# A two-layer graph network on one core: last keys on both array halves, moments from every other row tile, score rows by transfers

## The chip, the cores and the metric

The kernel runs on one core of a Trainium2 chip. The metric is device time of one execution in microseconds, the median of several runs. The engines are named as in the profile: PE is the matrix engine (PEld its weight loads, which can lie beside matmuls), DVE the vector engine, ACT the scalar engine, POOL the general engine, SP the engine whose queue issues most transfers. Each engine works through its own queue in order.

## The reference, cut to what matters

There are N = 3327 nodes with 256 features. The adjacency is dense in memory and mostly zeros.

```python
# layer 0: h = relu(layernorm(x)), then
R = adj + eye; R = R / R.sum(-1)
for n in range(2):
    logits = (Xa @ W1.T @ W2.T) @ (Xa @ W3.T).T          # queries and keys have 64 features
    probs  = softmax(logits)
    A  = probs kept from the largest down while the sum of those before is < 0.9, renormalized
    Xf = R @ Xf
    Xa = A @ Xa
    Z += Xf @ U1[n].T + Xa @ U2[n].T
x = x + layernorm(h + Z)
# layer 1: h = relu(layernorm(x)), hp = h @ W as 4 heads of 64
e    = leaky_relu(s[:, None] + d[None, :], 0.2)          # s, d: one score per node and head
attn = softmax(where(adj > 0, e, -inf))
x = x + elu(attn @ hp)
```

## The kernel before

Rows are cut into NT = 26 tiles of 128 (the last has 127 real rows, NP = 3328 with padding). Everything is float32; a float32 matmul shows as two records in the trace, a transpose as one. No order is written by hand: `Plan` (line 470) holds every piece of work with its engine, an assumed length, a rank (due time), what it needs, and which buffers it takes and gives. `Plan.order` (line 497) plays this through once: a free engine takes the ready piece of the lowest rank whose buffers are free. The pieces are then issued in the order found, each on its engine's queue. So any changed piece or length gives a new order everywhere.

The stages are these.

Preparation (`prepare`, line 1094): each row tile is loaded, normalized, transposed and projected into keys and queries (`wqk`). Keys lie in `kt`, transposed, 64 features on one half of the partitions; `half_of` (line 620) puts four tiles on the one half, the next four on the other, and so on. A row's queries lie in `qq` on both halves. So two logits matmuls of 64 partitions each can work on both halves of the array at once. Tiles 24 and 25, the last, are both on half 0. `project_u` (line 1149) multiplies by U1 ahead of the sums.

`moments` and `keys_summed` (lines 725, 1087): the sum and second moment of the keys, from which a row's mean and variance of logits follow. For each of 26 key tiles: a transpose (L733), an ACT copy (L737), a matmul of 65 columns (L742), two DVE additions into `gk` (L754). `scaled` divides by N, `stats` (line 758) takes each row's mean and variance.

Steps n = 0 and 1, ranks 0 and 30: per row tile, `search` (line 1350) with class `Row` (line 816) computes logits in two pieces (columns 0 to 2047, and 2048 to 3326 as a pair of 512 and one matmul of 255 on half 0, L845), exponentials on ACT (L856) into a buffer `e` of the pool of four, a first threshold from the moments, and two (step 0) or three (step 1) counts over the row (L893) that move the threshold. The number of counts is fixed. Then come a window, a sort and the choice on DVE. `attention` (line 1402) transposes `e` and multiplies (L1016, L1028). Column 3327 of `e`, the padding, is set to zero by POOL (L833) when the buffer is opened. `full` (line 1417) multiplies the row tile of R (loads of four adjacency tiles into one of four buffers `at`, L1049; matmuls L1060 from `main` or `c`); it is the filler of PE's queue. `finish1` (line 1162) makes the next step's keys, `finish2` (line 1251) the second layer's features and scores: `main[:, t]`, `sd`, `qd`, `low`. `failures` (line 1331) marks rows whose choice can't be trusted; one such row makes the whole program run again on the slow path `general`.

Neighbour stage (`attend_neighbours`, line 1440, ranks 60 to 99): four blocks b of W = 832 destination nodes. For each of the 26 source tiles j: the adjacency is loaded (L1513), turned into a bf16 mask in an `et` buffer (L1523, L1524), DVE multiplies the larger of two exponentials by the mask for each of four heads (L1535) into one of six buffers (four `e`, two in the memory of `rhs`), and PE multiplies (products L1551, denominators L1565, three tiles at a time). The scores of the destination nodes are broadcast to all partitions (`broadcast`, L1473 and L1477): for each tile and head a transpose of the score column seen as 128 equal columns, then an exponential into `both`, which lies in the memory of `c` and so needs all full sums of step 1 done (`opened`). Each block ends in `leave` (L1605, L1608), transposes (L1626), division, elu and the store.

## Time and profile before

| | us |
|---|---|
| median of 3 runs | 2272.42 (2270.28 to 2273.19) |
| profiled execution | 2271.77 |
| its span | 2269.9 |
| PE busy | 2207.6 |
| DVE busy | 1618.2 |
| ACT busy | 1480.0 |
| POOL busy | 915.3 |

A line of the profile's groups names the line of the kernel, the engine, the operation, what is written and read, how often, and then busy time, the mean of one in ns, and the idle time just before it with what ended that. Matmuls overlap, so the mean of one is longer than the distance from one to the next; the latter is what a queue can gain. Seen over the span, the preparation takes the first 60 us, step 0 lies up to some 940, step 1 up to some 1757, then the neighbour stage until 2247.6 and the output's end.

### The profile page before, as it was taken

The page shows a single profiled execution, that of the slowest core. Times are in us where ns is not written, and L with a number is a line of the kernel's source. Part 1 is how long each engine was busy: PE and PEld are TensorE (multiplying, and loading weights), DVE is VectorE, ACT ScalarE, POOL GpSimd, SP SyncE. Part 2 cuts the span into 40 slices and gives each one's busy share as a digit, 9 for nine tenths or more (in the row PEclk, how much of TensorE's full clock was granted, in tenths as well). Part 3 has the DMA queues.
Part 4 walks back from the last instruction along what each step waited for, and adds up shares of the span by engine and source line. Part 5 has one row for each costly group of instructions (what it writes and reads, how often), then busy time and mean ns, then how long its engine had stood idle before and what let it go on. Part 6 is the DMA issues. An engine that isn't in the chain of part 4 may idle for free. (4 is left out here: it accounts for less than half of the span.)

```text
span 2269.9 us, 36125 instructions
## 1 busy us (share of the span) xinstructions
PE 2207.6 (97%) x11956; PEld 1547.5 (68%) x11956; DVE 1618.2 (71%) x4273; ACT 1480.0 (65%) x2849; POOL 915.3 (40%) x2263
## 2 busy tenths in 40 slices
PE   7999999999999999999999999999999999999997
PEld 5477778777877778877878777878788433343332
DVE  5576656557565562277878898678776898989895
ACT  5766686677666851478887877777872646565553
POOL 6455555546533540256646656665561000000000
PEclk9999999999999999999999999999999999999998
DMA  3011221212212222531222122222222443434341
GB/s 98 20 37 53 83 69 53 64 51 61 74 48 74 69 82 76 183 86 54 65 57 73 56 61 70 70 75 75 67 74 78 119 118 107 120 106 120 102 126 42
DMA packets 189653, 176.96 MB, mean 78 GB/s; under 512 B 14866, under 2 KB 145808, under 8 KB 189328
## 3 DMA queue, kind: packets, MB, share of 16 engines
q1 hardware_dynamic: 187472, 173.30, 26.3%
q8 instruction: 96, 1.57, 0.3%
q10 hardware_dynamic: 1984, 1.26, 0.2%
q14 instruction: 101, 0.83, 0.1%
HBM read 157.66 MB, written 15.89 MB: 76 GB/s over the span
## 5 line engine op out<-in xcount | busy, mean ns | idle before, releaser
L1028 PE MATMUL acca<-rhs,et 128*128 128x256 f32 x2704 | 621.2, 380 | 0.8 <-ACT et L1021 0.8
L893 ACT ACTIVATE junk<-e,sc 128x3327 fp8e5<-128x3327 f32 x182 | 559.1, 3072 | 59.1 <-POOL sc L938 57.8
L1028 PEld LDWEIGHTS acca<-rhs,et 128*128 128x128 f32 x2704 | 498.5, 190 | 63.8 <-ACT et L1021 2.6
L1060 PE MATMUL accf<-main,at 128*128 128x257 f32 x1352 | 314.0, 382 | 4.9 <-DMA at<-in_adjt_dram 4.6
L1060 PE MATMUL accf<-c,at 128*128 128x256 f32 x1352 | 313.4, 382 | 4.8 <-ACT f L1067 4.7
L1535 DVE SCALAR_TENSOR_TENSOR e<-c,low,et 128x832 f32<-128x832 f32 x288 | 289.0, 1076 | 16.3 <-ACT e L1605 9.7
L1060 PEld LDWEIGHTS accf<-c,at 128*128 128x128 f32 x1352 | 250.2, 190 | 54.8 <-issue 14.1
L1060 PEld LDWEIGHTS accf<-main,at 128*128 128x128 f32 x1352 | 250.7, 191 | 47.1 <-issue 8.2
L1021 ACT COPY et<-px 128x512 f32<-128x512 f32 (+1 forms) x364 | 193.6, 553 | 133.3 <-PE acca L1028 72.5
L948 DVE SCALAR_TENSOR_TENSOR y<-e,sc 128x1664 f32<-128x1664 f32 x104 | 206.6, 1987 | 96.3 <-POOL sc L935 63.8
L953 DVE MAX8 cands<-y 128x8 f32<-128x208 f32 x832 | 242.7, 361 | 3.7
L1003 DVE SCALAR_TENSOR_TENSOR e<-e,thr 128x832 f32<-128x832 f32 x208 | 212.6, 1080 | 1.7
L1551 PE MATMUL pl<-e,main 128*64 128x416 f32 x1152 | 212.0, 516 | 0.1
L856 ACT ACTIVATE e<-pl 128x1024 f32<-128x1024 f32 x208 | 179.1, 863 | 45.6 <-PE pl L845 45.3
L1016 PE MATMUL px<-ident,e 128*128 128x128 f32 x1352 | 193.5, 275 | 7.6 <-ACT et L1021 4.5
L1524 ACT ACTIVATE et<-at 128x512 bf16<-128x512 f32 (+1 forms) x208 | 114.5, 550 | 127.6 <-DVE e L1535 82.4
L1016 PEld LDWEIGHTS px<-ident,e 128*128 128x128 f32 x1352 | 160.4, 141 | 51.6 <-issue 12.5
L845 PE MATMUL pl<-kt,qq 64*128 64x512 f32 (+1 forms) x728 | 184.1, 588 | 0.1
L1551 PEld LDWEIGHTS pl<-e,main 128*64 128x64 f32 x1152 | 79.8, 137 | 122.2 <-issue 102.2
L1535 DVE SCALAR_TENSOR_TENSOR rhs<-c,low,et 128x832 f32<-128x832 f32 x128 | 129.2, 1073 | 0.0
L845 PEld LDWEIGHTS pl<-kt,qq 64*128 64x128 f32 x728 | 70.9, 185 | 82.3 <-issue 76.5
L1523 ACT ACTIVATE at<-at 128x512 f32<-128x512 f32 (+1 forms) x208 | 112.1, 539 | 4.3 <-DMA at<-in_adjt_dram 4.2
(486 smaller groups left out, 2834.3 us busy)
## 6 DMA issues: line engine op xcount, KB each, us to landing
at<-in_adjt_dram SPq DMA_DIRECT2D x416, 256.0 KB, 2.7
at<-in_adjt_dram SPq DMA_DIRECT2D x104, 192.0 KB, 3.0
at<-in_adjt_dram SPq DMA_DIRECT2D x52, 128.0 KB, 2.1
ys<-ystage SPq DMA_DIRECT2D x26, 256.0 KB, 2.2
rhs<-in_x_dram SPq DMA_DIRECT2D x26, 128.0 KB, 2.9
ystage<-in_x_dram SPq DMA_DIRECT2D x26, 128.0 KB, 2.0
base<-ys SPq DMA_DIRECT2D x26, 128.0 KB, 2.2
x1s<-ystage SPq DMA_DIRECT2D x26, 128.0 KB, 1.7
```

The lines of the kernel that those rows point to most:

```text
L845: T.matmul(pl[:, r, :m], qq[half, self.i, :], kt[half, 512 * k : 512 * k + m], start=True, stop=True,)
L856: S.activation(self.e[:, 1024 * k : 1024 * k + pl.shape[1]], pl, AF.Exp, accum_out=(self.p0, self.p1, self.p2, self.p3)[k],)
L893: S.activation(junk[:, :N], self.e[:, :N], fn, bias=t, scale=-1.0, accum_out=dst, saturate=False)
L948: V.scalar_tensor_tensor(self.y[:, : hi - lo], self.e[:, lo:hi], self.up, self.e[:, lo:hi], ALU.is_lt, ALU.mult, accum_out=(self.h0, self. ...
L953: V.max(self.cands[:, o // PIECE, :], self.y[:, o - lo : min(o + PIECE, hi) - lo])
L1003: V.scalar_tensor_tensor(piece, piece, self.thr[:, o : o + 1], piece, ALU.is_gt, ALU.mult)
L1016: T.transpose(pt[:, k, :], self.e[:, j * P : (j + 1) * P], ident)
L1021: S.copy(self.et[g][:, :m, :], self.pt.pop(g)[:, :m, :])
L1028: T.matmul(self.acc, et[:, j - 4 * g, :], rhs[self.n][:, j, :], start=(j == 0), stop=(j == NT - 1))
L1060: T.matmul(self.acc[:, : self.w], self.at[j // JC][:, j % JC, :], self.src[:, j, : self.w], start=(j == 0), stop=(j == NT - 1),)
L1535: V.scalar_tensor_tensor(held["e"][:, k, :], extra["both"][b % 2][:, k, :], low[:, j, k : k + 1], held["mask"], ALU.max, ALU.mult,)
L1551: T.matmul(q["acc"][a][k * FH : (k + 1) * FH, c, :C], main[:, j, h * FH : (h + 1) * FH], held["e"][:, h, c * C : (c + 1) * C], start=(j == 0),
```

## The change

Last keys: tile 25 goes to half 1 (`side`), so that the last 255 logits of a row are 128 on half 0 beside 127 on half 1. The padding column is written by a matmul of one column (`none`), 32 ones by -1000, whose exponential is zero; the POOL memset goes. The exponentials read the two banks as a strided pair. The planner's length of the second logits piece falls from 1.6 to 1.4.

Moments: only the even tiles are summed, and the scale is 1 / (13 x 128).

Score rows: `spread_heads` transposes the scores of 6 or 7 tiles at once, takes the exponential, and stores 26 small row pieces to a DRAM tensor `highs`; `broadcast` becomes two transfers a block that read two heads each into all 128 partitions. Block 0 and 2 use the memory of `qq` for them, blocks 1 and 3 the first half of `c`, and the second half of `c` becomes a seventh buffer for exponents.

First tiles: source tiles 0 and 1 of block 0 have their adjacency in the memory of `kt` and their masks in that of `junk`, once all logits and counts of step 1 are done.

The check of a row: `m`, the number of equals kept, moves from `sc` to `met`, and a window whose smallest piece maximum equals the next value fails only where `m` is not zero.

```diff
+    highs = spill.tile([H, NP], F32, name="highs")
+    def side(t):
+        return 1 if t == NT - 1 else t // 4 % 2
     def half_of(t):
-        r = t // 4 % 2
-        lo = t // 8 * 512 + t % 4 * P
+        r = side(t)
+        lo = t // 8 * 512 + (t % 4 * P if t < NT - 1 else 0)
...
-        kt = wpool.tile([P, 4 * 512 - 256], F32, name="kt")
+        kt = wpool.tile([P, 3 * 512 + P], F32, name="kt")
+        none = wpool.tile([P, P + 2], F32, name="none")
+        GP.memset(none, 0.0)
+        GP.memset(none[DA : DA + 32, :P], 1.0)
+        GP.memset(none[DA : DA + 32, P:], -1.0e3)
...
-                GP.memset(self.e[:, N:], 0.0)
+                self.m = met[:, 5, self.i : self.i + 1]
...
-                w = min(1024, N - 1024 * k)
+                w = 512 if k < 3 else P
                 for r in range(2):
-                    m = min(512, w - 512 * r)
-                    if m > 0:
...
+                    m = min(w, N - 1024 * k - w * r)
+                    half = slice(r * DA, r * DA + DA)
+                    T.matmul(pl[:, r, :m], qq[half, self.i, :], kt[half, 512 * k : 512 * k + m], start=True, stop=True)
+                    if m < w:
+                        T.matmul(pl[:, r, m:w], none[half, :P], none[half, P : P + w - m], start=True, stop=True)
...
-            g = keys_summed(
+            g = t % 2 == 0 and keys_summed(
...
+            V.tensor_tensor(one, met[:, 1], met[:, 3], ALU.is_equal)
+            V.tensor_scalar(two, met[:, 5], 0.0, None, ALU.not_equal)
+            V.tensor_mul(one, one, two)
+            V.tensor_add(b, b, one)
...
             def open_heads():
-                extra["both"] = halves_of("c", None)
+                both = wpool.tile([P, NT, P], F32, name="qq").rearrange("p t d -> p (t d)")
+                extra["both"] = [both.rearrange("p (h w) -> p h w", h=H)]
+                extra["at"] = wpool.tile([P, 2 * W], F32, name="kt").rearrange("p (k w) -> p k w", k=2)
+                extra["m"] = scr.tile([P, NP // 2], BF16, name="junk").rearrange("p (k w) -> p k w", k=2)
+            def open_heads2():
+                both, e = halves_of("c", None)
+                extra["both"].append(both)
+                extra["e"] = [e]
...
+            opened = [plan.put("SP", 0.02, 59.0, open_heads, needs=[logits_done, counted], lag=0.0)]
+            opened.append(plan.put("SP", 0.02, 59.0, open_heads2, needs=[fulls, opened], lag=0.0))
+            def spread_heads(t0, t1):
+                def turn():
+                    held["ps"] = ps_x.tile([(t1 - t0) * H, P], F32, name="px")
+                    T.transpose(held["ps"], sd[:, 0, t0:t1, :].rearrange("p t h -> p (t h)"), ident)
+                def exps():
+                    held["rows"] = small.tile([7 * H, P], F32, name="rows", bufs=1)[: (t1 - t0) * H]
+                    S.activation(held["rows"], held["ps"], AF.Exp, scale=1.0 - ALPHA)
+                def store():
+                    for t in range(t0, t1):
+                        nc.sync.dma_start(
+                            highs[:, t * P : (t + 1) * P], held["rows"][(t - t0) * H : (t - t0 + 1) * H, :]
+                        )
...
+            cuts = (0, 7, 13, 20, NT)
             def broadcast(b, rank):
                 lo, hi = b * W, (b + 1) * W
-                    def turn(t=t, held=held):
-                        held["pb"] = ps_x.tile([P, H, P], F32, name="px")
-                        for k in range(H):
-                            T.transpose(held["pb"][:, k, :], sd[:, 0, t, k : k + 1].to_broadcast([P, P]), ident)
...
+                got, after = [], [spread[: b + 1], opened[b % 2], used_heads[b % 2]]
+                for a in range(2):
+                    def fetch(a=a):
+                        nc.sync.dma_start(
+                            extra["both"][b % 2][:, 2 * a : 2 * a + 2, :],
+                            highs[2 * a : 2 * a + 2, lo:hi].partition_broadcast(P),
+                        )
...
+                    def load_first(j=j):
+                        for t0, t1, w in ((0, W // P, P), (W // P, W // P + 1, W % P)):
+                            nc.sync.dma_start(
+                                extra["at"][:, j, t0 * P : (t1 - 1) * P + w].rearrange("p (i q) -> p i q", q=w),
+                                adjt[t0:t1, :, j, :w].rearrange("i p q -> p i q"),
+                            )
+                    def mask_first(j=j, held=held):
+                        held["mask"] = extra["m"][:, j, :]
+                        S.activation(extra["at"][:, j, :], extra["at"][:, j, :], AF.Relu)
+                        S.activation(held["mask"], extra["at"][:, j, :], AF.Sign)
...
-                            k = j % 6
+                            k = j % 7
...
+                    if b == 0 and j < 2:
+                        loads, own = plan.put("SP", 0.2, rank, load_first, needs=[opened[0]], lag=4.0), []
+                        m_ = plan.put("ACT", 1.8, rank, mask_first, needs=[loads])
...
-                lambda: V.tensor_scalar(gk[:, : DA + 1], gk[:, : DA + 1], 1.0 / N, None, ALU.mult), needs=[sums],
+                lambda: V.tensor_scalar(gk[:, : DA + 1], gk[:, : DA + 1], 1.0 / (NT // 2 * P), None, ALU.mult), needs=[sums],
```

## The prediction

> **What bounds the kernel now.** I read the page's busy table first, then stretches of the span, then the chain that ended last, then single engines in order of time around the places that the change touches.
>
> ```profile
> PE 2207.6 (97%) x11956; PEld 1547.5 (68%) x11956; DVE 1618.2 (71%) x4273; ACT 1480.0 (65%) x2849; POOL 915.3 (40%) x2263
> ```
>
> The matrix engine (PE) is busy 97% of the span and no other engine is over 71%. The stretches say where it is not:
>
> ```profile
> 0.00:60.00 60.00, 44.43 (x256) 33.51 (x256) 31.75 (x130) 34.77 (x114) 36.14 (x123) 0.97 0.35 101
> 1560.00:1600.00 40.00, 40.00 (x200) 32.30 (x198) 29.21 (x96) 31.68 (x51) 20.79 (x53) 1.00 0.21 60
> 1757.00:1771.00 14.00, 8.87 (x48) 6.42 (x47) 6.20 (x17) 10.40 (x24) 1.85 (x5) 0.76 0.48 138
> 1800.00:2000.00 200.00, 199.79 (x1472) 76.07 (x1467) 188.68 (x208) 106.76 (x246) 0.00 (x0) 1.00 0.40 115
> ```
>
> The columns are the stretch, its length, busy time of PE, weight loads, DVE, ACT and POOL, then PE clock, DMA share and GB/s. PE has no gap inside a step (second line: 40.00 of 40), so there a microsecond of PE work removed is a microsecond of span. It has gaps in the preparation and at the seam between step 1 and the neighbour stage (8.87 of 14.00). In the neighbour stage DVE is close behind it (188.68 against 199.79), so there the relief ends early. The chain shows the seam and the beat of that stage:
>
> ```profile
> 1749.44 7.78 PE accf L1060 x36
> 1765.16 0.91 PE px L1473 x4
> 1787.51 8.53 PE pl L1551 x48
> 1796.04 0.84 PE acca L1565 x8
> 1800.36 8.53 PE pl L1551 x48
> ```
>
> The last full sum ends at 1757.24. The first steady group of three neighbour tiles starts at 1787.51 and the next at 1800.36: 12.86 us for three tiles, 4.29 each. DVE's own pace for a tile's four products is faster:
>
> ```profile
> 1799.36 10.05 DVE L1535 SCALAR_TENSOR_TENSOR e<-c,low,et 128x832 f32<-128x832 f32 x10
> 1809.31 8.06 DVE L1535 SCALAR_TENSOR_TENSOR rhs<-c,low,et 128x832 f32<-128x832 f32 x8
> ```
>
> Ten start in 9.95 us, 0.995 each and 3.98 a tile.
>
> The profiled execution took 2271.77 us (span 2269.9 and 1.87 around it), the median of the runs is 2272.42, 0.65 above. I sum against 2271.77 and add 0.65. Less than 0.2% (4.5 us) can't be told from no change.
>
> **Part 1: the seam and the neighbour stage.** Before, PE spends 1757.24 to 2247.6, 490.4 us, from the last full sum to the end of the last denominator. The work that stays: 26 tiles in eight groups of three and one of two, 8 x 12.86 + 8.57 = 111.45 a block, 445.8 for four. Row tile 25's last transposes and projection: 1.1. The output transposes of three blocks (the fourth's lie after 2247.6), 21 at 0.48 (L1626 at 1896.61, next group at 1897.09): 10.1. What goes is the score broadcast, 112 transposes at L1473:
>
> ```profile
> 1886.11 1.09 PE L1473 MATMUL px<-ident,sd 128*128 128x128 f32 x8
> 1887.13 4.41 PE L1551 MATMUL pl<-e,main 128*64 128x416 f32 x24
> ```
>
> Eight take 1.02 us, so 112 take 14.3; its 28 ACT exponentials (0.59 each) go too, but ACT is busy 106.76 of 200 there and gives nothing.
>
> Stalls. The blocks started with their first product at 1887.1, 2008.5 and 2129.1, and the last ended at 2247.6: 121.4, 120.6 and 118.5. Less 111.45, less seven output transposes (3.4), less seven broadcasts in blocks 1 and 2 (3.7), that leaves 2.8, 2.0 and 3.7 in which products wait for DVE, which also does 7 x 1.0 of output work at each boundary. Some broadcasts ran inside such waits (1910.21, 1913.06), so removing them uncovers a wait; the seventh buffer for exponents lets DVE run 4 us further ahead. Ends: 0 and 5 a block; I take 3, as measured: 9.
>
> Start. Before, the products could not start before the full sums freed `c` for the scores; the first was at 1771.47, 14.2 us after 1757.24, and three tiles were done at 1787.43. After, scores lie in `qq`, the first two neighbour tiles in `kt`, their masks in `junk`, all free once the last row's logits and counts are done. DVE has nothing from 1740.2 to 1757.6 but 0.6 us, room for four tiles; PE has row 25 and full sums there, so nothing is lost. Tile 2 still needs an `at` buffer that full sums hold (its load was issued at 1752.9). Ends: 0 and 14 (as before); I take 3, because tiles 0 and 1 cover 5.7 us of product work and the third was masked by 1762. The first two tiles' loads stay two transfers each and their masks become two ACT instructions instead of four over the same columns: nothing. Their exponents go into DVE's in-order queue among row 25's last pieces, each of which they can hold up by 2 us (a pair of products); PE covers that with the 7.8 us of full sums shown above, and main tile 25 is read 100 us later. Sum 445.8 + 1.1 + 10.1 + 9 + 3 = 469.0: gain 21.4, ends 4 and 33.
>
> Against it: four small transposes, each with a switch as before (0.11 to 0.27 each): 1.0 lost. SP issues 26 more stores of 0.34 us (L1280's issue), 8.8 in all, four bursts of 2.4, each behind a wait for an ACT exponential; queued behind them are loads of full sums. SP waited 1038.5 us for PE to free those buffers, so it is ahead. Four buffers hold 6.9 us of full-sum work: 0 to 3 lost, I take 1. The eight broadcast fetches (852 KB each) are due a block later; nothing waits for them unless they hold up `at` loads (rival 3).
>
> **Part 2: last keys on both halves.**
>
> ```profile
> 928.71 1.55 PE L845 MATMUL pl<-kt,qq 64*128 64x512 f32 x6
> 930.19 11.57 PE L1060 MATMUL accf<-main,at 128*128 128x257 f32 x52
> ```
>
> The second logits piece of a row takes 1.48: a pair of 512 columns at 0.85 (weight loads at 929.24, 929.67 mark the passes), 255 columns at 0.425 and 0.2 of switch. Split over both halves the 255 become 128 beside 127: 0.213, saving 0.212. Added is a one-column matmul that writes the padding column, on the half that just ran, with its own two weight loads. The trace has no such matmul. Nearest is the moments product, 65 columns, two records in 0.17 where its columns alone need 0.108: 0.06 too long. Ends for the fill: 0.02 and 0.25 (two loads of 0.107, the pitch of the transposes, fully bare, and some issue). I take 0.11, between the two: 52 x 0.10 = 5.2 gained, ends -2 and 10.
>
> The row before the rule: 128x256 attention matmuls run eight in 1.73 us, 0.216 each, which is their columns alone, while each weight load takes 190 ns: loads are hidden behind matmuls on the same rows. The Trainium skill (TensorE: Matmul & The Clock Gate, sections "The mechanism" and "LDWEIGHTS (loading the stationary operand)") says that a weight load overlaps a running matmul only when its row group differs, and puts 128 columns at 128 / 1.2 ns; as an estimate from that page, two bare loads are 0.21 us, the split would save nothing, and the total would be 5 us higher. This trace's rows disagree, and I go by them.
>
> Three memsets for the fill's operands join POOL's queue ahead of the preparation, some 0.1 to 0.2 each by the memsets of the trace: 0 to 0.5 lost, hidden behind the first loads, which land at 10 us and later. The memset of the padding (52 x 0.099 on POOL) goes. DVE waited 30.3 us for it in eight places, ACT once for 1.5; PE had other work, which covers it: 0, ends 0 and 3.
>
> **Part 3: moments from every other row tile.**
>
> ```profile
> 903.76 0.27 PE L733 MATMUL px<-ident,kq 128*128 128x128 f32 x1
> 903.87 1.90 PE L1060 MATMUL accf<-main,at 128*128 128x257 f32 x8
> 905.61 0.33 PE L742 MATMUL px<-kk 127*128 127x65 f32 x2
> 905.78 1.95 PE L1060 MATMUL accf<-main,at 128*128 128x257 f32 x8
> ```
>
> One tile costs 0.11 + 0.17 = 0.28 of PE. Thirteen fewer in step 0's finish: 3.6. DVE loses 13 x 0.32 there and idled 103.8 us waiting for these products; in its in-order queue that wait stands ahead of other rows' work, so fewer is no loss: gain ends 3 and 5. In the preparation PE waits for ACT until 46 us, then does twelve tiles without such a wait until the first logits at 59.9; six of them lose 0.28 of PE and an ACT copy of 0.27: 1.7 to 3.3, and PE's gap there is filled by later projection work only in part. I take 2, ends 0 and 5.
>
> `failures` gains four small DVE instructions of 0.19 a step, ahead of which no row waits: nothing; the cover is PE's backlog, bare it would be 1.5.
>
> **Sum.** 21.4 - 1.0 - 1.0 + 5.2 + 3.6 + 2.0 = 30.2. 2271.77 - 30.2 + 0.65 = 2242.2. The whole order is written anew by the planner; between 60 and 1650 us PE idles some 22 us by such stretches, most of it at the seams of the steps, and a new order can move a third of that either way: 8.
>
> **Rivals.** 1: DVE becomes the bound and the early start fails, because exponents of the first tiles wait for `e` buffers that rows 22 to 25 hold, and for masks. For: DVE at 188.68 of 200. Against: DVE's 104 x 3.98 + 28 x 1.0 = 442 is below 469. Part 1 then gives its lower end, 4: 2272.42 - (4 - 2 + 5.2 + 3.6 + 2) = 2259.6.
>
> 2: the PE work is hidden anyway: moments and logits shortened, but rows wait for ACT (52 rows x about 3.4 counts of 3.07) and DVE instead. For: ACT waits little in steps. Against: 40.00 of 40 for PE with full sums as filler. Steps then give 0, part 1 stays: 2272.4 - 19.4 = 2253.0.
>
> 3, slower: the broadcast fetches stall the neighbour stage. Place: SP's queue in blocks 0, 1, 2, where a fetch waits for the last exponents of the block before, and the `at` loads are queued behind it. Price: a transfer of 1472 KB (`qq<-qqs`) took 9.5 us, so a pair of 852 KB takes 11; the longest wait of SP for the masks was 13.1. Both bare, less the two tiles that `at` holds (8.6), are 15.5 a block, 46.5 in all: 2288.7. It decides from 10 us a block on (30.2 / 3). Against: the loads run at 115 GB/s of DMA share 0.40, and the fetch is due 60 us before its use.
>
> 4: the halved sample gives poorer first thresholds, `failures` marks a row, and the whole general path runs. The number of evaluations is fixed, so a poorer guess costs no time below that point; no row prices it, thousands of us.
>
> **How the numbers follow.** Main case 0.60, rival 1 0.13, rival 2 0.12, a mix near no change 0.04, rival 3 and other losses at seams 0.09, rival 4 0.02. Main case's own range is 2222 to 2260 (part 1 at half its ends, and the 8 of the order). Low 2218: part 1 at 33, logits at 10. High 2264 takes in rival 1 with the order's loss. Faster 0.85, same 0.04, slower 0.11.
>
> **What would show it.** Right: no 112 transposes; first product of the neighbour stage at or before the end of the last full sum; its blocks near 118 us; second logits piece near 1.38; 26 fewer moment products. Wrong: products waiting for DVE for over 5 us at each boundary, `at` masks waiting for DMA, or PE's gaps at the step seams grown.

## The result, and the profile after

| | before | after |
|---|---|---|
| median, us | 2271.69 (2270.28 to 2273.19) | 2239.47 (2238.08 to 2240.89) |
| profiled execution | 2271.77 | 2240.52 |
| its span | 2269.9 | 2238.6 |
| PE busy | 2207.6 | 2177.3 |

The ratio is 0.9858 (95% interval 0.9841 to 0.9875): 32.2 us or 1.4% faster, against 30.2 predicted. (The median of before has one run more in it here than in the prediction.)

The busy table of the changed kernel:

```profile
PE 2177.3 (97%) x11978; PEld 1537.8 (69%) x11978; DVE 1615.0 (72%) x4229; ACT 1455.7 (65%) x2795; POOL 925.1 (41%) x2214
```

PE is still 97% busy. Its busy time fell by 30.3 us and its idle time only by 1 (62.3 to 61.3). That fits a bound that is one engine's work, but the split must not be taken at its word: the ends of matmuls are modelled, so a product that waits for a late operand can count as busy.

Stretches of the changed kernel (length, then busy time of PE, weight loads, DVE, ACT and POOL, PE clock, DMA share, GB/s):

```profile
1560.00:1600.00 40.00, 39.69 (x208) 32.32 (x207) 33.17 (x107) 29.46 (x54) 28.39 (x57) 1.00 0.25 73
1800.00:2000.00 200.00, 198.64 (x1439) 74.30 (x1436) 179.50 (x211) 108.01 (x275) 0.00 (x0) 1.00 0.44 127
```

The steps are as full of PE work as before. In the neighbour stage PE fell from 199.79 to 198.64 of 200 and DVE from 188.68 to 179.50.

Where the time came from is read at four points that both traces have: the first logits of step 0, the first and the end of the last logits of step 1, and the end of the last denominator.

| | before | after | gained by then |
|---|---|---|---|
| first logits of step 0 | 59.9 | 59.1 | 0.8 |
| first logits of step 1 | 915.3 | 907.4 | 7.9 |
| end of the last logits of step 1 | 1665.3 | 1656.7 | 8.6 |
| end of the last denominator | 2247.6 | 2216.4 | 31.2 |

So 22.6 of 31.2 us come after the last logits. Two things must be known of such marks. The first logits come anywhere from 58.8 to 60.7 in the twelve kernels here that prepare the moments from half of the tiles, so the 0.8 in the first row can't be told from nothing. And the changed kernel has less old work left when its last logits end: 180 records of full sums instead of 196, two transposes and four projections fewer. At 0.216, 0.11 and 0.22 us each that is 4.6 us, an estimate from the pitch of such records, so about 18.0 of the 22.6 belong to the later stages and 13.2 to what lies ahead.

The timeline of PE in the changed kernel at the seam:

```profile
1718.23 10.63 PE L1074 MATMUL accf<-c,at 128*128 128x256 f32 x48 [1.71 <-ACT f L1081]
1728.79 1.62 PE L1608 MATMUL pl<-e,main 128*64 128x416 f32 x8
1730.33 0.88 PE L1030 MATMUL px<-ident,e 128*128 128x128 f32 x6
...
1741.24 4.48 PE L1042 MATMUL acca<-rhs,et 128*128 128x256 f32 x20
1745.66 5.81 PE L1608 MATMUL pl<-e,main 128*64 128x416 f32 x32
```

The first neighbour product (L1608) follows the last full sum (L1074) with no gap, 14.2 us nearer to it than before. It even comes before the last row's attention (L1030, L1042), with more products between its pieces. From there the chain of the changed kernel has the beat of the old one, and shows the last pairs of products of the four blocks:

```profile
1758.79 8.53 PE pl L1608 x48
1771.65 8.53 PE pl L1608 x48
...
1850.76 5.74 PE pl L1608 x32
...
1970.18 5.74 PE pl L1608 x32
...
2089.04 5.74 PE pl L1608 x32
...
2207.90 5.74 PE pl L1608 x32
```

Three tiles still take 12.86 us. From one block's last pair to the next it is 119.42, 118.86 and 118.86 us; before it was 121.39, 121.20 and 119.03. So the blocks themselves gave 2.0, 2.3 and 0.2. The larger part lies ahead of the first block's last pair: from the end of the last logits to that pair it took 212.2 us and now takes 194.1, 18.1 less, the 4.6 of earlier work among them.

What is left at a boundary between blocks is seen in the timelines of DVE and PE of the changed kernel:

```profile
1877.37 4.04 DVE L1592 SCALAR_TENSOR_TENSOR c<-c,low,et 128x832 f32<-128x832 f32 x4
1881.33 0.42 DVE L1705 SCALAR_TENSOR_TENSOR ystage<-ystage 128x256 f32<-128x256 f32 x1
1881.78 0.43 DVE L1706 SCALAR_TENSOR_TENSOR ystage<-ystage,f 128x256 f32<-128x256 f32 x1
```

```profile
1881.46 1.62 PE L1608 MATMUL pl<-c,main 128*64 128x416 f32 x8
1884.11 4.60 PE L1608 MATMUL pl<-rhs,main 128*64 128x416 f32 x16 [1.03 <-DVE rhs L1592]
```

DVE puts the output work of the block that has ended (L1705, L1706) between the exponents of the new one (L1592), and PE then waits for exponents. This reading led to the last two experiments.

The second logits piece of a row in the changed kernel, from its first matmul to the next work:

```profile
920.86 1.35 PE L856 MATMUL pl<-kt,qq 64*128 64x512 f32 x8
922.04 0.28 PE L864 MATMUL pl<-none 64*128 64x1 f32 x2
922.25 11.57 PE L1074 MATMUL accf<-main,at 128*128 128x257 f32 x52
```

It takes 1.40 us where it took 1.48, in all 52 rows alike: 0.085 less, 4.4 us in all.

### The profile page after: what moved, and what is told of

It is laid out like the page before. It is cut to its first block, busy times and chain, and to the rows that moved or that the text cites. A ratio compares the mean times of both kernels' runs of the same rounds, so it can differ in the third digit from the quotient of the medians.

```text
span 2238.6 us, 36037 instructions
## 1 busy us (share of the span) xinstructions
PE 2177.3 (97%) x11978; PEld 1537.8 (69%) x11978; DVE 1615.0 (72%) x4229; ACT 1455.7 (65%) x2795; POOL 925.1 (41%) x2214
## 4 chain that ended last, share of the span: by engine, by line
PE 75%; ACT 8%; POOL 6%; DVE 5%; issue 3%; DMA 1%; SPq 0%; ACTq 0%; POOLq 0%; DVEq 0%
PE acca L1042 20%; PE accf L1074 20%; PE pl L1608 12%; PE px L1030 6%; PE pl L856 6%; ACT junk L907 5%; PE acca L1622 3%; PE accf L1622 3%; PE px L1217 2%; POOL sc L920 1%; PE px L1312 1%; PE px L1169 1%; DVE cands L967 1%; DVE y L962 1%; ACT et L1035 1%
## 5 line engine op out<-in xcount | busy, mean ns | idle before, releaser
L1042 PE MATMUL acca<-rhs,et 128*128 128x256 f32 x2704 | 619.4, 380 | 1.0 <-ACT et L1035 0.9
L1042 PEld LDWEIGHTS acca<-rhs,et 128*128 128x128 f32 x2704 | 499.9, 191 | 64.4 <-ACT et L1035 2.9
L1074 PE MATMUL accf<-c,at 128*128 128x256 f32 x1352 | 313.5, 382 | 5.5 <-ACT f L1081 5.5
L1074 PE MATMUL accf<-main,at 128*128 128x257 f32 x1352 | 312.0, 382 | 5.6 <-DMA at<-in_adjt_dram 5.3
L962 DVE SCALAR_TENSOR_TENSOR y<-e,sc 128x1664 f32<-128x1664 f32 x104 | 209.0, 2010 | 149.0 <-POOL sc L949 147.0
L1074 PEld LDWEIGHTS accf<-main,at 128*128 128x128 f32 x1352 | 252.8, 191 | 47.9 <-issue 6.5
L1074 PEld LDWEIGHTS accf<-c,at 128*128 128x128 f32 x1352 | 250.0, 190 | 47.7 <-ACT f L1081 10.3
L1581 ACT ACTIVATE et<-at 128x448 bf16<-128x448 f32 (+1 forms) x204 | 112.2, 550 | 137.3 <-DVE e L1592 81.5
L1030 PE MATMUL px<-ident,e 128*128 128x128 f32 x1352 | 191.2, 275 | 9.2 <-DVE gk L766 4.5
L1030 PEld LDWEIGHTS px<-ident,e 128*128 128x128 f32 x1352 | 159.5, 141 | 51.8 <-issue 15.3
L1608 PE MATMUL pl<-e,main 128*64 128x416 f32 x1024 | 187.2, 515 | 0.0
L856 PE MATMUL pl<-kt,qq 64*128 64x512 f32 (+1 forms) x832 | 173.5, 535 | 0.0
L1608 PEld LDWEIGHTS pl<-e,main 128*64 128x64 f32 x1024 | 71.0, 137 | 107.3 <-issue 92.0
L1592 DVE SCALAR_TENSOR_TENSOR e<-c,low,et 128x832 f32<-128x832 f32 x128 | 128.6, 1072 | 8.2 <-PE accf L1622 3.9
L1592 DVE SCALAR_TENSOR_TENSOR e<-qq,low,et 128x832 f32<-128x832 f32 x120 | 120.5, 1074 | 2.6 <-ACT e L1668 2.0
L1580 ACT ACTIVATE at<-at 128x448 f32<-128x448 f32 (+1 forms) x204 | 109.8, 538 | 11.9 <-DMA at<-in_adjt_dram 11.8
```

The source lines that it names most:

```text
L856: T.matmul(pl[:, r, :m], qq[half, self.i, :], kt[half, 512 * k : 512 * k + m], start=True, stop=True,)
L962: V.scalar_tensor_tensor(self.y[:, : hi - lo], self.e[:, lo:hi], self.up, self.e[:, lo:hi], ALU.is_lt, ALU.mult, accum_out=(self.h0, self. ...
L1030: T.transpose(pt[:, k, :], self.e[:, j * P : (j + 1) * P], ident)
L1042: T.matmul(self.acc, et[:, j - 4 * g, :], rhs[self.n][:, j, :], start=(j == 0), stop=(j == NT - 1))
L1074: T.matmul(self.acc[:, : self.w], self.at[j // JC][:, j % JC, :], self.src[:, j, : self.w], start=(j == 0), stop=(j == NT - 1),)
L1592: V.scalar_tensor_tensor(held["e"][:, k, :], extra["both"][b % 2][:, k, :], low[:, j, k : k + 1], held["mask"], ALU.max, ALU.mult,)
```

## The experiments

The theory to be tested: the gain is PE work taken away at its full price (broadcast transposes, moments, part of the logits), and, as a smaller part, the early start of the neighbour stage. The rivals were that the PE work was hidden beside DVE, that only the reordering by the planner moved the time, and that the transfers hold up the queue of SP. Each ratio below is against the kernel before on the same chip. "Above the changed kernel" is the difference of its ratio from 0.9858, times 2272. One such ratio is uncertain by some 3.4 us and the difference of two by some 5, so differences of 2 to 3 us are weak evidence, and the text leans on the traces where it can. Where a difference of medians is given too, it is against 2239.47.

**The logits as before.** Tile 25 goes back to half 0, with its matmul of 255 columns and the memset of the padding. The planner's length stays as changed.

```diff
-        return 1 if t == NT - 1 else t // 4 % 2
+        return t // 4 % 2
...
+                GP.memset(self.e[:, N:], 0.0)
...
-                    if m < w:
-                        T.matmul(pl[:, r, m:w], none[half, :P], none[half, P : P + w - m], start=True, stop=True)
```

> The changed kernel with the last 255 keys back on one half, the padding memset back on POOL, and the planner's lengths left as changed, so the order of work stays the same. Theory (PE bounds the steps, each PE microsecond removed counts): the second logits piece goes from 1.39 to 1.48 us, 52 rows, so 4 to 6 us slower than the changed kernel (2239.5): 2243 to 2246. Rival (hidden behind ACT and DVE in the steps): within 1 us of 2239.5. A rival by which the memset's waits matter: over 2248.

Measured: 2243.91 us, ratio 0.9869 (0.9854 to 0.9884), 2.5 above the changed kernel, 4.4 by medians. The last logits start at 1658.2 where the changed kernel has them at 1655.3; but 1.6 of these 3.0 us are there at the first logits already (60.65 against 59.06), within the scatter named above. So the split yields some 2.5 to 4.4 us, below or at the low end of what was expected, and by the time alone it isn't resolved.

**The planner's length alone.** All of the change stays but the length that the planner assumes for the second logits piece.

```diff
-                    "PE", 2.1 - 0.7 * g, rank - 2.5, logits, ...
+                    "PE", 2.1 - 0.5 * g, rank - 2.5, logits, ...
```

> The changed kernel with only the planner's assumed length of the logits pieces put back to 2.1 and 1.6. No instruction changes, only their order. It prices reordering by itself. Theory: within 3 us of 2239.5 either way. If it moves by 8 us or more, the parts of the change can't be told from the order they bring about.

Measured: 2242.14 us, ratio 0.9867 (0.9852 to 0.9882), 2.0 above, 2.7 by medians. No instruction differs, only the order. Yet the first logits of step 1 come at 900.17 instead of 907.43, and the last start at 1654.12 instead of 1655.26: a step can be 7 us ahead at its seam and give nearly all of it back within the next. A gain that is read at such a seam is no gain of the kernel yet.

**All moments.**

```diff
-            g = t % 2 == 0 and keys_summed(
+            g = keys_summed(
...
-                kk = held["kk"] = kks[t // 2 % 2]
+                kk = held["kk"] = kks[t % 2]
...
-  1.0 / (NT // 2 * P)
+  1.0 / N
```

> The changed kernel with moments from all 26 tiles again. Theory: 13 x 0.28 us of PE in step 0's finish and about 1 us before the first logits (59.9 against 59.1): 4 to 6 us slower than 2239.5. Rival (the work is covered): within 1.5 us. Rival that waits of DVE for the products stood in rows' way: 8 us or more slower.

Measured: 2246.92 us, ratio 0.9886 (0.9871 to 0.9902), 6.4 above, 7.4 by medians. PE's busy time is 2186.3, 9.0 higher. The first logits come at 60.1 instead of 59.1, the last ones start at 1661.5 instead of 1655.3. The thirteen moments of each of two passes are 7.3 us of PE work (26 x 0.28), and 6.4 to 7.4 came back, so they were on the path at nearly their full price, and the rival that PE's work in the steps is hidden falls. How much of it belongs to the preparation isn't resolved: 60.1 lies within the scatter of the first logits.

**The broadcast on PE again.** The score rows are made as before the change, by transposes of broadcast columns and exponentials, but into the new buffers. Own buffers for the first tiles, moments and logits stay as changed.

```diff
+                        for k in range(H):
+                            T.transpose(held["pb"][:, k, :], sd[:, 0, t, k : k + 1].to_broadcast([P, P]), ident)
...
-                        nc.sync.dma_start(
-                            extra["both"][b % 2][:, 2 * a : 2 * a + 2, :],
-                            highs[2 * a : 2 * a + 2, lo:hi].partition_broadcast(P),
-                        )
```

> The changed kernel with the scores broadcast by 112 PE transposes and 28 ACT exponentials again, into the new buffers, with the early start, the first tiles' own buffers and the seventh exponent buffer kept. Theory: 14.3 us of PE come back, 1 to 2 us of small transposes and stores go, and about 3 us lie in waits for DVE at block boundaries: 8 to 13 us slower than 2239.5. Rival (DVE bounds the neighbour stage, the transposes lie beside it): 0 to 3 us slower. Rival (transfers hold up the loads): faster than 2239.

Measured: 2261.08 us, ratio 0.9948 (0.9934 to 0.9962), 20.5 above: much more than expected. The chain of this kernel has the last pairs here:

```profile
1864.95 5.74 PE pl L1592 x32
...
1986.78 5.74 PE pl L1592 x32
...
2108.53 5.74 PE pl L1592 x32
...
2227.96 5.74 PE pl L1592 x32
```

The blocks take 121.83, 121.75 and 119.43: 2.4, 2.9 and 0.6 longer than in the changed kernel, as expected. The other 14.1 us are there when the first block's last pair comes (1864.95 against 1850.76). The timeline of PE in this kernel at the seam shows them:

```profile
1746.64 1.04 PE L1502 MATMUL px<-ident,sd 128*128 128x128 f32 x8
...
1750.94 1.78 PE L1502 MATMUL px<-ident,sd 128*128 128x128 f32 x8 [1.87 <-ACT qq L1506]
1754.44 0.69 PE L1303 MATMUL px<-ident,xa 128*128 128x128 f32 x2 [1.71 <-ACT qq L1506]
...
1759.45 1.62 PE L1592 MATMUL pl<-e,main 128*64 128x416 f32 x8
```

Broadcasts of rank 59.5 stand behind all full sums in PE's order. So the first product comes 13 us after the last of them, in spite of the new buffers, and PE waits for ACT between the transposes. The early start needs free buffers, and also scores that are there without PE.

**The same, with block 0's broadcast earlier.** This tells the price of the transposes from that of their place.

```diff
-            ... broadcast(0, 59.5)
+            ... broadcast(0, 50.0)
```

> The changed kernel with the scores broadcast by PE again (20 us slower than the changed kernel), but block 0's broadcast ranked ahead of the last rows' work (50 instead of 59.5), so that it is done under PE's backlog and the early start is had. Theory A (of the 20 us, some 10 were the early start lost, the rest PE work): 8 to 12 us slower than 2239.5. Theory B (PE work and the switches alone cost 20): still 18 or more slower.

Measured: 2253.93 us, ratio 0.9919 (0.9905 to 0.9933), 13.9 above. Block 0's transposes now run at 1695 to 1702 among the full sums, and the first product starts at 1748.93. The place was worth about 6.6 (20.5 less 13.9), which the planner's rank alone can bring back. The 13.9 that stay are near the bare PE time of the transposes, 14.3. Block 0's last pair starts at 1857.96, 7.2 later than in the changed kernel, and the 56 transposes ahead of it are 7.1 at full price. Some 2.2 us of both figures are likely not the transposes' own: PE's clock in steps 0 and 1 is halved for longer here (see the logits below). The block periods are 121.78, 121.52 and 119.43: 2.4, 2.7 and 0.6 longer, where full price would be 3.6, 3.6 and 0. In the blocks, then, waits for DVE hide about a quarter of it. The first product comes 20 us later than in the changed kernel (1728.79) and still nothing is lost by that: PE has full sums and the last rows to do until then.

**Score rows and first tiles opened late.** The buffers are as in the change, but all of them wait for the full sums of step 1.

```diff
-            opened = [plan.put("SP", 0.02, 59.0, open_heads, needs=[logits_done, counted], lag=0.0)]
+            opened = [plan.put("SP", 0.02, 59.0, open_heads, needs=[logits_done, counted, fulls], lag=0.0)]
```

> The changed kernel with the score rows of block 0, the first tiles' loads and masks allowed only after all full sums of step 1, as before. Broadcast by transfers, seven buffers and the rest stay. Theory (the early start is worth what the seam lost before, 14 us from the last full sum to the first product, less what stays): 8 to 14 us slower than 2239.5, all of it before the first product. Rival (PE has other work at the seam, the gain is the 14.3 us of transposes alone): 0 to 3 us slower.

Measured: 2248.78 us, ratio 0.9894 (0.9879 to 0.9909), 8.2 above, as expected. The chain of this kernel has the same beat, 8.5 us later:

```profile
1859.25 5.74 PE pl L1608 x32
...
1978.44 5.74 PE pl L1608 x32
```

The first product starts at 1750.5. The block periods are those of the changed kernel (119.19 and 118.86), so the early opening is worth some 8 us, once, at the seam. The timeline of PE in this kernel shows what most of it is:

```profile
1741.98 0.69 PE L1030 MATMUL px<-ident,e 128*128 128x128 f32 x2 [4.61 <-ACT et L1035]
1742.46 3.62 PE L1042 MATMUL acca<-rhs,et 128*128 128x256 f32 x8
```

PE waits for 4.61 us, and the eight matmuls after it take 3.4 us where eight take 1.73 elsewhere. The granted clock is 0.50 from 1740.7 to 1747.6, with 5.6 us of PE work in that stretch, of which about half, 2.8, is lost. The changed kernel has no such stretch between 873 us and 2215.

**First tiles in the common buffers.** Only the early scores stay; tiles 0 and 1 use `at`, `et` and the mask buffers as all others.

```diff
-                    if b == 0 and j < 2:
+                    if False:
```

> The changed kernel with source tiles 0 and 1 of block 0 loaded and masked in the common buffers, whose release the full sums set. Early score rows stay. Theory (own buffers give PE 5.7 us of products while the common ones come free): 3 to 6 us slower than 2239.5. Rival (the score rows alone bring the early start): 0 to 1.5 us slower.

Measured: 2241.28 us, ratio 0.9862 (0.9847 to 0.9877), 0.9 above, 1.8 by medians. The first product comes only at 1743.5, but the first group of denominators at 1754.6, where the changed kernel has it at 1754.4. The products that the own buffers allow early lie in a stretch where PE has the last row's attention to do anyway; without them the order is turned round and the sum is the same. This part of the change can't be told from nothing.

**Six exponent buffers.**

```diff
-                            k = j % 7
+                            k = j % 6
```

> The changed kernel with six exponent buffers instead of seven. Theory (the seventh lets DVE run one tile further ahead over each of three block boundaries): 2 to 5 us slower than 2239.5, in the block periods (119.4, 118.9, 118.9 in the changed kernel). Rival (DVE's total work sets the boundary, not its run-ahead): 0 to 1 us slower.

Measured: 2242.55 us, ratio 0.9867 (0.9852 to 0.9882), 2.0 above. The block periods are 119.82, 119.03 and 119.03, longer by 0.40, 0.17 and 0.17. So 0.7 of it is the missing buffer in the blocks; whether the rest is the buffer or the new order stays open, as the planner's length alone moved as much.

**Each broadcast transfer issued twice.** The third rival said that fetches can hold up the queue of SP.

```diff
+                        for _ in range(2):
                             nc.sync.dma_start(
                                 extra["both"][b % 2][:, 2 * a : 2 * a + 2, :],
                                 highs[2 * a : 2 * a + 2, lo:hi].partition_broadcast(P),
                             )
```

> The changed kernel with every broadcast transfer issued twice into the same place (6.8 MB more in all). Theory (nothing waits for them but block 0's, which have room): 0 to 1.5 us slower than 2239.5. Rival 3 of the prediction in a small form (they hold up the loads): at least 3 us slower, with masks waiting for transfers at each block.

Measured: 2273.73 us, ratio 1.0002 (0.9993 to 1.0011). Eight transfers more cost 33 us, the whole gain, where next to nothing was expected. What SP waits for in this kernel (microseconds in all, times, longest):

```profile
SPq L1526 <- DMA qq<-highs: 25.1, 4, 8.6
...
SPq L1526 <- DMA c<-highs: 24.0, 4, 7.1
```

The second transfer writes where the first does, so SP waits until the first has landed, eight times, some 6 us each, 49.1 in all. The chain of this kernel at the seam shows what stands behind:

```profile
1705.29 5.34 DMA qq<-highs
...
1711.06 7.64 DMA qq<-highs
...
1719.63 6.83 DMA kt<-in_adjt_dram
1726.54 0.91 ACT kt L1565
...
1730.68 0.27 ACT f L1081
1730.99 12.45 PE accf L1074 x48
```

The adjacency of the first tiles (`kt`) is loaded late, ACT waits for it with the masks, and behind the masks in ACT's queue stands the copy (L1081) that frees the accumulator for the next full sum. PE stands still for 12.93 us, and the first neighbour product comes at 1743.36. At the boundaries the chain goes through both fetches and an `at` load in the same way. Behind each stall PE also runs at half the clock for a while, as after block 0 (stretch, its length, PE, weight loads, DVE, ACT, POOL, PE clock, DMA share, GB/s):

```profile
1884.90:1891.70 6.80, 6.16 (x20) 2.64 (x22) 1.22 (x4) 6.26 (x23) 0.00 (x0) 0.50 0.51 148
```

From the seam on there are four such stretches, with 16.7 us of PE work in them. Half of that, up to 8.3 of the 33 us, is what the clock can have cost.

The changed kernel has a small form of the stall at the seam. Its timeline of ACT:

```profile
1713.78 0.90 ACT L1564 ACTIVATE kt<-kt 128x832 f32<-128x832 f32 x1 [2.82 <-DMA kt<-in_adjt_dram]
...
1716.11 0.88 ACT L1564 ACTIVATE kt<-kt 128x832 f32<-128x832 f32 x1
1717.02 0.90 ACT L1565 ACTIVATE junk<-kt 128x832 bf16<-128x832 f32 x1
1717.82 0.35 ACT L1081 COPY f<-accf 128x256 f32<-128x256 f32 x1
```

That copy ends PE's gap of 1.71 shown at the seam. So the masks of the first tiles, late by their load, cost PE up to 1.7 us there. The fetches do little: the timeline of SP has two of them issued in 0.97 us, and block 2's in 2.36, after a wait of up to 4.0 for the last exponents of block 0:

```profile
1703.68 0.97 SPq L1525 DMA_DIRECT2D qq<-highs  x2
...
1843.07 2.36 SPq L1525 DMA_DIRECT2D qq<-highs  x2
```

SP waits 9.6 us for such exponents in three places, and ACT 11.8 us for `at` loads in five (longest 3.7), where it was 4.2 before. But the chain of the changed kernel at the block boundaries has exponents of DVE and no transfer. The mechanism of the third rival is real, then, and strong; in the change it stays too short to reach PE.

**The duplicates from POOL's queue.** The same eight transfers more, but issued by POOL, once the first ones are done.

```diff
+                    def again(a=a):
+                        nc.gpsimd.dma_start(
+                            extra["both"][b % 2][:, 2 * a : 2 * a + 2, :],
+                            highs[2 * a : 2 * a + 2, lo:hi].partition_broadcast(P),
+                        )
+                    f = plan.put("SP", 0.1, rank, fetch, needs=[after], lag=7.0 + 5.0 * a)
+                    got.append([f, plan.put("POOL", 0.1, rank, again, needs=[f], lag=10.0)])
```

> The changed kernel with every broadcast transfer issued a second time into the same place, now from POOL's queue, which has nothing else in the neighbour stage. The bytes are those of the doubled transfers on SP's queue (33 us slower than the changed kernel), but the wait of the second for the first stands in POOL's queue. Theory A (the price was SP's queue standing still, 14 us a group, with the loads behind it): 0 to 6 us slower than 2239.5. Theory B (the price was the bytes): 20 us or more slower, with masks waiting for transfers.

Measured: 2244.60 us, ratio 0.9873 (0.9857 to 0.9888), 3.4 above, 5.1 by medians. The same bytes (204 GB/s in the stretch from 1700 to 1750, where the changed kernel has 166) cost a tenth to a seventh of what they cost on SP's queue. So nearly all of the 33 us were the queue that stood still, with what followed from it. The traffic has a price too, but a small one: at the seam PE waits 3.83 us for an `at` load of a full sum here (before 1729.33), and has half the clock for 3.4 us after it.

**The output work spread over the next block.** This follows from the boundary shown above. The output work of blocks 0 to 2 gets ranks that rise through the next block, instead of one rank at its beginning.

```diff
+                    rr = r1 + (1.0 + 0.8 * (x0 // P) if b < 3 else 0.0)
...
-                        "PE", 0.4, r1 + 0.02, turn, ...
+                        "PE", 0.4, rr + 0.02, turn, ...
-                    a = plan.put("DVE", 0.2, r1, invert, ...
+                    a = plan.put("DVE", 0.2, rr, invert, ...
```

The fetch, the elu, the additions and the store get `rr` in the same way.

> The changed kernel with the output work of blocks 0 to 2 (transposes, division, elu, store) ranked over the following block, a tile for each 2 to 3 source tiles, instead of all at its start. DVE's pace of 3.98 us a tile against PE's 4.29 leaves 8 us a block, the output work on DVE takes 7. Theory (the 4 us of stall left in each of three block periods of 119 us are DVE's output work in one lump): periods fall to 115 to 117, 6 to 10 us faster than 2239.5. Rival (the held exponent buffer costs what the spreading gains): within 2 us.

Measured: 2233.97 us (2232.20 to 2236.05), ratio 0.9829 (0.9815 to 0.9843), 6.6 below the changed kernel, 5.5 by medians: the fastest of all kernels here. The timeline of PE in this kernel has the output transposes (L1689) three at a time between steady groups:

```profile
1863.27 5.81 PE L1608 MATMUL pl<-e,main 128*64 128x416 f32 x32
...
1872.53 0.88 PE L1622 MATMUL accf<-e,qd 128*32 128x416 f32 x8
1873.34 0.55 PE L1689 MATMUL px<-ident,e 128*128 128x128 f32 x3
```

Its chain has block 0's last pair at 1851.25 and block 3's at 2202.32, so the blocks take 117.02 on the average, 2.0 less than in the changed kernel's 119.05. Of the 4.2 us of stall that were left in a block 2.2 stay.

**Spread wider.** Ranks rise by 1.25 a piece instead of 0.8.

```diff
-                    rr = r1 + (1.0 + 0.8 * (x0 // P) if b < 3 else 0.0)
+                    rr = r1 + (1.0 + 1.25 * (x0 // P) if b < 3 else 0.0)
```

> The kernel with the output work spread over the following block (5.5 us faster than the changed kernel, periods 117.05), spread wider: a tile for every 3 to 4 source tiles instead of 2 to 3. Theory (what is left over the 111.45 of bare products and 3.4 of transposes is still DVE work bunched up): 1 to 2 us faster than 2234. Rival (the buffer that holds a block's output until its last transpose leaves DVE one buffer short for longer): 0 to 3 us slower than 2234.

Measured: 2235.83 us, ratio 0.9836 (0.9823 to 0.9849). Not faster than the spread before. The trace says a little slower: block 0's last pair comes at 1849.38 and block 3's at 2201.37, so a block takes 117.33 instead of 117.02. (That the profiled execution is none the less 0.9 shorter goes with the clock: this kernel has one stretch of 3.4 us at half the clock in step 0, the other has 10.2.) The theory that more distance removes the rest falls.

Added up, the parts undone one at a time give 2.5 (logits) + 6.4 (moments) + 20.5 (broadcast by transfers) + 0.9 (own buffers) + 2.0 (seventh buffer) = 32.3, beside 32.2 for the whole. That it comes out so exactly is chance, with some 5 of uncertainty in each; by medians the same sum is 38.4. So it shows which parts are large, and doesn't prove that none is unseen. The early opening (8.2) is not a further term: the broadcast on PE loses its early start too.

## Why the prediction was right

The sum gave 2242.2, the time is 2239.47. The bound was read rightly: PE's own work in the steps, and PE with DVE close behind in the neighbour stage. That the sum came within 2 us of the gain is luck in part, since terms of it that were off by several us cancel. Point by point:

**The seam and the neighbour stage** (predicted 21.4, less 1.0 for small transposes and 1.0 for SP's stores, so 19.4): measured 22.6 from the last logits to the last denominator, of which about 4.6 is old work done earlier, so 18.0. The prediction measured from the last full sum; that mark doesn't serve after the change, since the last row's attention now comes behind it. The size holds. Inside it:

- *The broadcast's 14.3 us of transposes:* with block 0's broadcast ranked early, having them on PE costs 13.9, some 2.2 of it likely the clock in the steps. The step was right in the main.
- *The stalls (3 a block, predicted to stay as measured):* a block takes 119.05 on the average, and 111.45 for tiles and 3.4 for output transposes leave 4.2. So the transposes taken out of blocks 1 and 2, 3.6 each, gave 2.0 and 2.3, and the rest uncovered a wait for DVE. The prediction named this mechanism and then took none of it: 1.2 a block too low.
- *The start (3 left of 14):* the first product comes at the moment when the last full sum ends. That nearness alone proves nothing, as the first product comes 13.6 us after it with the first tiles in common buffers, in nearly the same time; what counts is that PE's gaps at the seam are down to 1.71 and 0.88. Opening early is worth 8.2 by its own experiment. Part of this is the clock, for which the prediction had no term, although its own row of the seam shows 0.76: before, 4.06 us of PE work lay in 6.8 us at half the clock (1760.9 to 1767.7), so 2.0 were lost, and the changed kernel has none of that there. What else the prediction had no term for is that the early start rests on the transfers too, since transposes of that rank would run behind the full sums (6.6 us).
- *The first tiles in their own buffers:* the prediction let the start rest on them ("because tiles 0 and 1 cover 5.7 us of product work"). They bring 0.9, not told from nothing, and their masks in ACT's queue hold up PE by up to 1.7. The prediction looked at DVE's queue for such a hold-up and not at ACT's. The scores in `qq` do it.
- *The seventh buffer:* 0.7 in the block periods. It gave little against the stalls, which are DVE's output work at the boundaries and not a lack of buffers.
- *SP's 26 stores:* taken as 1.0. No run prices them; the two gaps of PE at the seam end with ACT's copy and with DVE's last choice, not with a store.

**The logits** (predicted 5.2): the second piece takes 1.40 where 1.38 was predicted, so 4.4 less for 52, and both pieces of all rows together take 174.6 us of PE, each from its first record to the next other work, where the undone kernel needs 178.6: 4.0. By the time it is 2.5 (4.4 by medians), and from the first logits to the last ones the two traces differ by 1.4 alone. PE's idle time between 60 and 1700 us is 22.6 before, 24.8 after, and 24.7 with the logits undone, so new gaps don't take the rest. The clock does. The changed kernel has two stretches at the end of step 0 in which half the clock is granted, the kernel with the logits undone has one (third line):

```profile
811.50:818.30 6.80, 4.75 (x11) 3.83 (x12) 2.80 (x6) 0.00 (x0) 0.73 (x2) 0.50 0.45 165
869.50:872.90 3.40, 3.40 (x11) 2.86 (x10) 0.00 (x0) 0.58 (x1) 0.00 (x0) 0.50 0.00 0
816.90:820.30 3.40, 3.40 (x8) 2.74 (x9) 0.97 (x4) 0.00 (x0) 0.57 (x2) 0.50 0.33 126
```

Each comes with a gap of PE: 5.34 us ahead of 813.55, 2.09 ahead of 869.31, and 5.02 in the undone kernel. In the second stretch eight attention matmuls take 3.2 us (first line), right after it 1.7:

```profile
870.00 3.34 PE L1042 MATMUL acca<-rhs,et 128*128 128x256 f32 x8
...
874.06 1.89 PE L1042 MATMUL acca<-rhs,et 128*128 128x256 f32 x8
```

So about half of PE's busy time in such a stretch is lost: 4.1 us in the changed kernel and 1.7 in the other. These 2.4 taken from 4.0 leave 1.6, beside the 1.4 measured. That the split brought the longer stretches about isn't shown: the kernel with the output spread wider has the same logits and one stretch of 3.4 us.

The fill's price was the unknown (ends 0.02 and 0.25, taken 0.11). Of the 0.212 that the split saves, 0.085 is left, so fill and reloading cost 0.13 a piece. Its two weight loads show 188 ns each in the records; fully bare at the transposes' pitch they alone would have been 0.21. The Trainium skill (TensorE: Matmul & The Clock Gate, "The mechanism") has a weight load overlap a running matmul only on other row groups, by which the split was to save nothing. The fill uses the same half as the matmul just ahead of it, and still 0.085 was saved: the measurement decides against the sum by that rule, as the attention rows did in the prediction. The same section also lets a load go ahead into a background weight buffer, which would fit the rows; how much of each load lay under a matmul these runs don't show. The memset's 0 holds: DVE's wait ahead of the window pieces did not fall.

```profile
L962 DVE SCALAR_TENSOR_TENSOR y<-e,sc 128x1664 f32<-128x1664 f32 x104 | 209.0, 2010 | 149.0 <-POOL sc L949 147.0
```

The memset is no longer among its releasers, but the wait is 149.0 in all, now mostly for the search's steps on POOL, where it was 96.3 before; no gain is seen.

**The moments** (predicted 3.6 + 2.0 = 5.6): 6.4 by their own experiment. The sum was a bit small. Its two terms can't be told apart: the first logits differ by 0.8 and 1.0, less than they scatter, and from there to the first logits of step 1 the experiment is 5.0 slower, where 3.6 was predicted and the order alone moves that mark by 7. One reading was wrong, in a term of 0 to 0.5: before the change the first row tile had landed at 3.00 us, not at 10 or later, so the first loads don't cover the three memsets as was said. No run prices them.

**The order** (8 either way): the gain up to the first logits of step 1 was 7.9 (8.2 by the terms), and step 1 then added 0.7 where its logits should have added 2.6; the 4.6 of other work that was done by then is the likely reason. The planner's length alone moved the time by 2.0, the seam by 7. A bound of 8 was wide enough. One end of the stated range doesn't follow from its terms: rival 1 with the order's loss is 2259.6 + 8 = 2267.6, above the high end of 2264.

**The rivals.** DVE as the bound: DVE's waits do set the block boundaries (4.2 a block), but the early start did not fail, so its 2259.6 was not reached. PE's work hidden in the steps: refuted by the moments. Fetches that stall SP's queue: the mechanism works, with 49.1 us of waiting and 33 us of time where it is forced. In the change SP waits at most 4.0 us for the exponents that a fetch needs, and no transfer is in the chain of the block boundaries. Of the signs of being wrong, the masks did wait longer for transfers (11.8 instead of 4.2 in all) and PE's gaps up to 1700 us grew from 22.6 to 24.8, too little to turn the sum. The general path did not run.

## What to carry to other kernels

Where one engine is 97% busy and no other is near, its removed work comes back at nearly its full price; where another is close behind, about three quarters of it did here. Read the gain at the end of the program all the same, since an order written anew can show 7 us at a seam and give them back. A gap of the busy engine can cost more than itself, since the clock was halved behind several of them here, so look at the granted clock of the stretch behind it before you call a part of the gain lost. To start a stage early, every operand must be there early: free buffers bring nothing while the scores still come from the busy engine, at a rank behind its other work. After such a change look at the next wait, here the output work gathered at the block boundaries: spread over the next block it gave another 5.5 to 6.6 us, with no instruction removed.

## What was not expected of the hardware

A queue that issues transfers in order is a resource of its own. Eight more transfers of 852 KB cost 33 us on SP's queue, where each had to wait for one to the same place, and 3.4 to 5.1 on POOL's, with the same bytes. In the first case two in-order queues, SP's and then ACT's, carried the delay on to PE. Starved at the seam, PE showed a granted clock of 0.86 between 1700 and 1750 us (1.00 in the changed kernel):

```profile
1700.00:1750.00 50.00, 36.87 (x175) 30.38 (x174) 28.00 (x82) 14.71 (x25) 8.26 (x22) 0.86 0.51 162
```

The record of the clock has it at 0.5 from 1721.0 to 1734.7, across most of the gap of 12.93 us and 3.7 us of PE work. The 48 matmuls after the gap took 12.44 us where they take 10.63 in the changed kernel, so the lower clock cost 1.8 beyond the gap itself.

The clock's records hold 0.5 or 1.0 and nothing between in all traces here, and the stretches at 0.5 between 60 us and the last denominators are 3.4, 6.8 or 13.7 us long. All kernels have at least one of them at the end of step 0. How long a gap must be to set one off isn't settled by these runs: one of 3.4 us followed a gap of 2.09.
